# Layer-0 experts in units of 256 rows and halves of 128 rows

## The chip, the cores and the metric

The kernel runs on one core of a Trainium2 chip. A time is the device time of one execution in microseconds (us); the time of a kernel is the median of its timed runs. One more execution is recorded by the hardware profiler; the profile's lines come from that one. Its engines are PE (TensorE matmuls; PEld is its weight load), DVE (VectorE), ACT (ScalarE), POOL (GpSimd) and SP (SyncE, which here only issues DMAs).

## The reference, cut to what matters

The whole kernel computes two graph layers on 1250 nodes of 512 features. Each has a graph product, an attention part and a mixture of experts. Only the experts of layer 0 are concerned here:

```python
logits = jnp.einsum('btd,ed->bte', h, w_r) + b_r
topk_vals, topk_idx = jax.lax.top_k(logits, K)
gates = jax.nn.softmax(topk_vals, axis=-1)
hf = h.reshape(B * T, d)
hid = jax.nn.gelu(jnp.einsum('nd,edf->nef', hf, W1) + b1, approximate=False)
expert_stack = jnp.einsum('nef,efd->ned', hid, W2) + b2
gathered = jnp.take_along_axis(expert_stack, idx_flat[:, :, None], axis=1)
mixed = jnp.sum(gathered * gates_flat[:, :, None], axis=1).reshape(B, T, d)
return x + mixed
```

There are E = 8 experts, K = 2 for each node, d = 512 and a hidden width of 2048, all in float32. So 2500 (node, expert) pairs have to pass through a 512x2048 map, a gelu and a 2048x512 map, each with the weights of its own expert. Which expert a pair takes is known only while the kernel runs.

## The kernel before, in words

**Routing and planning.** The function `tile_graph_layers` is one long program. After the first graph product, `route` (called per 125 rows) writes the normalised rows to the DRAM table `hrow` and the logits to `lg`. Then the planning block (lines 655 to 751) runs once. `top2` gives the two experts of each row as one-hot masks `oh` and the gates. A matmul with a triangular matrix gives `pos`, the rank of each row within its expert; its last slice holds the row count of each expert. `un` holds the units of each expert (its rows divided by UT = 256, rounded up), their running sum, and the sum before. `eu` gives each unit its expert, and a flag that says whether this differs from the expert of the unit before. Both go as integers into `plan`, together with the number of units. `row` is the place of a pair: 256 times the first unit of its expert, plus its rank. From `row`, the tables `hi` and `lo` and twenty matmuls into `pslot` make `sf` and `slot`: for each block of 128 places, the row to fetch, the gate, and the row to add to. NB = 34 blocks. DVE does nearly all of this in small operations, and PE waits for `hi` before `pslot`.

**A unit.** There are up to NU = 17 units; the first NU0 = 10 run always (2500 pairs need at least 10), the others in nested branches `tc.If(n_units > u)`. `unit(u)` does the following:

- `weights(u)` (lines 801 to 810): SP reads the expert and the flag from `plan`, fetches the bias, and issues eight conditional loads of 1 MB, `ew1[0]`, `ew2[0]`, `ew1[1]`, `ew2[1]` and so on. Both maps have one set of four buffers each, so a load waits until the unit before has used that quarter.
- First map (line 820): for each 128 of the 2048 hidden columns, four matmuls accumulate in PSUM. The weights are stationary, the 256 turned rows `hu` are moving. ACT applies bias and gelu (line 821) into `hd`.
- `counts` (lines 168 to 191) for some of NG = 54 groups. This is work of layer 1, put here: each group counts edges of the graph. DVE and ACT make one-hot tiles (`sh`, `los`, four buffers), PE multiplies six pairs of them into `pa` (one PSUM bank, "acc"), ACT copies `pa` to `sa` (three buffers), and POOL adds `sa` into the DRAM table `adj` with an indirect accumulating DMA. Units 0 to 9 carry 5 or 6 groups each.
- `turn(u + 1)` transposes the next unit's rows (line 795), `fetch(u + 2)` gathers rows from `hrow` (line 783, POOL).
- Second map (line 829): for each quarter and each 128 hidden columns, two matmuls (one per 128 rows), with `hd` stationary and 512 columns of `ew2` moving, into two PSUM tiles `pye`.
- The two results are multiplied by the gates (lines 835 and 837) into `yo` and added to the DRAM table `xrow` by accumulating DMAs of POOL (line 838).

The order on each engine is set when the program is built, by priority and by a model of the engines: work of a later statement fills the gaps of an earlier one, except that nothing moves in or out of a branch. After the units, layer 1 begins: SP loads `adj` (`ad`, lines 868 to 881) and `xrow` (line 903), and PE transposes and multiplies.

Of the kernel before, what the change touches and what calls it, by code (L numbers as in the profile page):

```python
# [10 lines left out]
F32 = mybir.dt.float32  # L11
F16 = mybir.dt.float16
I32 = mybir.dt.int32
AF = mybir.ActivationFunctionType
OP = mybir.AluOpType
AX = mybir.AxisListType
# [3 lines left out]
N = 1250  # L20
D = 512
P = 128
R = 125
NT = N // R
# [14 lines left out]
EPS = 1e-5  # L39
E0, F0 = 8, 2048  # L40
UT = 2 * P
NU = (2 * N - E0) // UT + E0
NU0 = -(-2 * N // UT)
E1, F1 = 6, 341
EA = 5
FA = EA * F1
# [6 lines left out]
def tile_graph_layers(ctx: ExitStack, tc: tile.TileContext, i: dict, out: bass.AP):  # L53
    nc = tc.nc
    V, S, T, G = nc.vector, nc.scalar, nc.tensor, nc.gpsimd
# [18 lines left out]
    def mm_tile(name):  # L74
        return ps_tile("mm", name)

    def in_tile(name):
        return ps_tile("in", name)

    def tr_tile(name):  # L80
        return ps_tile("tr", name)
# [19 lines left out]
    ident = cst.tile([P, P], F32, name="ident")  # L101
# [51 lines left out]
    hrow = dram.tile([N, D], F32, name="hrow")  # L153
    xrow = dram.tile([N + P, D], F32, name="xrow")
# [38 lines left out]
    with ExitStack() as s0:  # L193
# [78 lines left out]
        for t in range(NT):  # L272
# [40 lines left out]
        base = ec.tile([P, 2, NG], F32, name="base")  # L313
# [203 lines left out]
        for b, blocks in ((3, ((3, 0), (3, 1), (3, 2))), (1, ((1, 0), (2, 0), (2, 1)))):  # L517
            pt = tr_tile("pgl")
# [12 lines left out]
        for a in range(4):  # L531
            pt = mm_tile("pt1")
# [12 lines left out]
        for c in range(4):  # L545
            pt = tr_tile("pwq")
# [23 lines left out]
        for a in range(4):  # L570
            pt = mm_tile("pmap")
            for c in range(4):
                T.matmul(pt, wqn[:, c, a * P:(a + 1) * P], U[:, c, :], start=c == 0, stop=c == 3)
            f = 1.0 / (math.sqrt(N) * cout)
# [74 lines left out]
    with ExitStack() as s3:  # L649
        fc = pool(s3, "fc")  # L650
        fw = pool(s3, "fw", bufs=2)
# [6 lines left out]
        oh, gw2 = top2(nc, fc, lg[:R], gates[:R], R, NT, E0, softmax=True)  # L658
# [10 lines left out]
        for t in range(NT):  # L669
# [6 lines left out]
        pos = fc.tile([P, NT + 1, E0], F32, name="pos")  # L676
# [1 line left out]


        KU = -(-N // UT)  # L680
        stp = fc.tile([P, KU], F32, name="stp")
        G.iota(stp, pattern=[[UT, KU]], base=0, channel_multiplier=0, allow_small_or_imprecise_dtypes=True)
        cmp_ = fc.tile([P, E0, KU], F32, name="cmpu")
        V.tensor_tensor(cmp_, pos[:, NT, :, None].to_broadcast([P, E0, KU]), stp[:, None, :].to_broadcast([P, E0, KU]),
                        op=OP.is_gt)
        un = fc.tile([P, 3, E0], F32, name="un")
        V.tensor_reduce(un[:, 0, :], cmp_, AX.X, OP.add)
        V.tensor_copy(un[:, 1, :], un[:, 0, :])
        for e in range(1, E0):
            V.tensor_tensor(un[:, 1, e:e + 1], un[:, 1, e - 1:e], un[:, 0, e:e + 1], op=OP.add)  # L690
        V.tensor_tensor(un[:, 2, :], un[:, 1, :], un[:, 0, :], op=OP.subtract)

        ui = fc.tile([P, NU], F32, name="ui")
        G.iota(ui, pattern=[[1, NU]], base=0, channel_multiplier=0, allow_small_or_imprecise_dtypes=True)
        cme = fc.tile([P, NU, E0], F32, name="cme")
        V.tensor_tensor(cme, ui[:, :, None].to_broadcast([P, NU, E0]), un[:, 1, None, :].to_broadcast([P, NU, E0]),
                        op=OP.is_ge)
        eu = fc.tile([P, 2, NU], F32, name="eu")
        V.tensor_reduce(eu[:, 0, :], cme, AX.X, OP.add)
        V.tensor_scalar(eu[:, 0, :], eu[:, 0, :], float(E0 - 1), None, op0=OP.min)  # L700
        V.memset(eu[:, 1, 0:1], 1.0)
        V.tensor_tensor(eu[:, 1, 1:], eu[:, 0, 1:], eu[:, 0, :NU - 1], op=OP.not_equal)
        plan = fc.tile([P, 2 * NU + 1], I32, name="plan")
        V.tensor_copy(plan[:, :2 * NU], eu.rearrange("p a u -> p (a u)"))
        V.tensor_copy(plan[:, 2 * NU:], un[:, 1, E0 - 1:E0])


        row = fc.tile([P, NT, E0], F32, name="row")
        V.scalar_tensor_tensor(row[:R], un[:R, 2, None, :].to_broadcast([R, NT, E0]), float(UT), pos[:R, :NT, :],
                               op0=OP.mult, op1=OP.add)  # L710
        rw_ = fc.tile([P, 2, NT, E0], F32, name="rw_")
        rf = fc.tile([P, 2, NT], F32, name="rf")
        for n in range(2):
            V.tensor_tensor(rw_[:R, n], oh[n][:R], row[:R], op=OP.mult)
            V.tensor_reduce(rf[:R, n, :], rw_[:R, n], AX.X, OP.add)
        ri = fc.tile([P, 2 * NT], I32, name="ri")
        V.tensor_copy(ri[:R], rf[:R].rearrange("p n t -> p (n t)"))
        NB = NU * UT // P
        part = fc.tile([P, 2, 2 * NT], I32, name="part")
        V.tensor_scalar(part[:R, 0, :], ri[:R], 7, None, op0=OP.arith_shift_right)  # L720
        V.tensor_scalar(part[:R, 1, :], ri[:R], P - 1, None, op0=OP.bitwise_and)
# [7 lines left out]
        q = [R, 2 * NT, NB]  # L729
        V.tensor_tensor(hi[:R, :, 1, :], bi[:R, None, :NB].to_broadcast(q), pf[:R, 0, :, None].to_broadcast(q),  # L730
                        op=OP.is_equal)
# [5 lines left out]
        for a in range(2 * NT):  # L737
# [3 lines left out]
                     stop=a == 2 * NT - 1)  # L741

        sf = fc.tile([P, 5, NB], F32, name="sf")
# [6 lines left out]
        slot = fc.tile([P, 2, NB], I32, name="slot")  # L750
# [15 lines left out]
        ew1 = [fc.tile([P, 4, 512], F32, name=f"ew1_{q}") for q in range(4)]  # L766
        ew2 = [fc.tile([P, 4, 512], F32, name=f"ew2_{q}") for q in range(4)]

        def value(n, engines, top):
            return nc.values_load(plan[0:1, n:n + 1], engines=engines, min_val=0, max_val=top,  # L770
                                  skip_runtime_bounds_check_because="worked out above, within these bounds")

        SPE = (mybir.EngineType.SP,)
# [23 lines left out]
            return hu  # L797

        def weights(u):
            e, new = value(u, SPE, E0 - 1), value(NU + u, SPE, 1)  # L800
            b1 = fw.tile([P, 16], F32, tag="b1", name="b1")
            nc.sync.dma_start(b1[:, None, :], i["L0_ffn_b1"][:, bass.ds(e, 1), :])
            for q in range(4):
                nc.sync.dma_start(
                    ew1[q], i["L0_ffn_W1"][bass.ds(e, 1), :, q * 512:(q + 1) * 512].rearrange("o (k p) f -> p (o k) f", p=P),
                    cond=new)
                nc.sync.dma_start(
                    ew2[q], i["L0_ffn_W2"][bass.ds(e, 1), q * 512:(q + 1) * 512, :].rearrange("o (k p) f -> p (o k) f", p=P),
                    cond=new)
            return b1  # L810

        def unit(u, hu, xu):
            b1 = weights(u)
            hd = []
            for q in range(4):
                hd.append(fw.tile([P, 4, UT], F32, tag="hd", bufs=6, name="hd"))
                for f in range(4):
                    ph = in_tile("phd")
                    for k in range(4):
                        T.matmul(ph[:, :UT], ew1[q][:, k, f * P:(f + 1) * P], hu[:, k, :], start=k == 0, stop=k == 3)  # L820
                    S.activation(hd[q][:, f, :], ph[:, :UT], AF.Gelu, bias=b1[:, 4 * q + f:4 * q + f + 1], scale=1.0)  # L821
            for g in range(u * NG // NU0, (u + 1) * NG // NU0 if u < NU0 else 0):
                counts(fk, g, code0, idx0, "acc")
            after = turn(u + 1, xu) if u + 1 < NU else None, fetch(u + 2) if u + 2 < NU else None
            py = [mm_tile("pye") for _ in range(2)]
            for q in range(4):
                for f in range(4):
                    for a in range(2):
                        T.matmul(py[a], hd[q][:, f, a * P:(a + 1) * P], ew2[q][:, f, :],  # L829
                                 start=q == 0 and f == 0, stop=q == 3 and f == 3)  # L830
            for a in range(2):
                yo = fw.tile([P, D], F32, tag="yo", bufs=3, name="yo")
                k = 2 * u + a
                if a:
                    S.mul(yo, py[a], sf[:, 1, k:k + 1])
                else:
                    V.tensor_scalar(yo, py[a], sf[:, 1, k:k + 1], None, op0=OP.mult)  # L837
                G.indirect_dma_start(  # L838
                    out=xrow[:, :], out_offset=bass.IndirectOffsetOnAxis(ap=slot[:, 1, k:k + 1], axis=0),
                    in_=yo, in_offset=None, compute_op=OP.add)  # L840
            return after

        hu, xu = turn(0, fetch(0)), fetch(1)
        for u in range(NU0):
            hu, xu = unit(u, hu, xu)
        n_units = value(2 * NU, mybir.ALL_ENGINES, NU)
        with ExitStack() as s4:
            for u in range(NU0, NU):
                s4.enter_context(tc.If(n_units > u))
                hu, xu = unit(u, hu, xu)  # L850
    sc_.close()

    with ExitStack() as s1:
        xp = pool(s1, "xp")
        XN = xp.tile([P, NT, D], F32, name="XN")
        with ExitStack() as s2:
            ap = pool(s2, "adj")
# [3 lines left out]
            with ExitStack() as s3:  # L861
# [4 lines left out]
                for d in range(NT):  # L866
# [7 lines left out]
                    for s0_ in range(0, NT, 4):  # L874
                        n = min(4, NT - s0_)
                        pt = tr_tile("pat")
# [78 lines left out]
        n = FA // P  # L955
# [318 lines left out]
```

## Time and profile before

| what | us |
|---|---|
| median of the timed runs (three: 2479.42, 2479.59, 2485.83) | 2479.59 |
| the profiled execution's own time | 2379.38 |
| its span, from first to last instruction | 2377.6 |
| first expert matmul starts | 782.8 |
| the last of the unconditional units ends on PE | 1396.6 |
| first of the conditional units starts its first map | 1399.3 |
| last expert result is made | 1573.1 |
| mean granted PE clock | 0.965 of full speed |

Both times are of the same kernel; the profiled execution is 100 us shorter than the median of the timed ones. In a line of the profile's groups, `out<-in` names the tiles, `128*128 128x512` the stationary and the moving operand of a matmul, `xN` the number of records, then busy us and mean ns of one, then the idle time of the engine just ahead of these instructions and what ended it. A float32 matmul of this kernel is recorded as two passes, so 832 records of line 829 are 416 matmuls, 32 for each of 13 units. A line of a timeline has start and duration in us, engine, source line, operation, names, and in brackets the idle time before it with its releaser. A line of the windows view has the stretch, its length, the busy time of PE, PEld, DVE, ACT and POOL, the granted clock, the busy share of the DMA engines and GB/s.

### The profile page before, as it was taken

How to read it: one execution, taken by the hardware profiler on the slowest of the kernel's cores; microseconds unless marked ns; L12 is line 12 of the kernel's file. 1: busy time of each engine (PE TensorE's matmuls, PEld its weight loads, DVE VectorE, ACT ScalarE, POOL GpSimd, SP SyncE). 2: the span in 40 equal slices, each digit the busy share in tenths (PEclk: the TensorE clock that was granted, in tenths of full speed). 3: DMA queues.
4: the chain of work that ended last, by engine and by line, in shares of the span. 5: the costliest groups of instructions: out<-in, count | busy, mean ns of one | idle time of the engine just before them, and what ended most of it. 6: DMA issues, size and time to landing. Idle time of an engine off the chain costs nothing. (4 is left out here: it accounts for less than half of the span.)

```text
span 2377.6 us, 29905 instructions
## 1 busy us (share of the span) xinstructions
PE 2220.0 (93%) x11524; PEld 1223.3 (51%) x11524; DVE 875.9 (37%) x1814; ACT 616.0 (26%) x1631; POOL 599.3 (25%) x535
## 2 busy tenths in 40 slices
PE   6889888899897999999999999979999999988999
PEld 4334333333464666666666656644446455443454
DVE  3588888888365212111111110023000124573000
ACT  1444444443121333333233321122111011122000
POOL 0577777777020112222222220000000000002000
PEclk9899999999996899999999999989999999989999
DMA  6687777777433656522652245433002030110000
GB/s 218 236 221 199 185 186 186 186 184 183 103 95 103 191 166 156 146 32 49 173 152 31 27 95 159 142 84 109 0 0 67 4 68 18 36 30 1 13 13 18
DMA packets 129004, 253.63 MB, mean 107 GB/s; under 512 B 21532, under 2 KB 52204, under 8 KB 127308
## 3 DMA queue, kind: packets, MB, share of 16 engines
q0 software_dynamic: 47536, 116.88, 21.9%
q1 hardware_dynamic: 78952, 129.64, 17.6%
q10 hardware_dynamic: 2356, 5.00, 0.8%
q8 instruction: 97, 1.59, 0.3%
q14 instruction: 63, 0.52, 0.1%
HBM read 245.60 MB, written 47.81 MB: 123 GB/s over the span
## 5 line engine op out<-in xcount | busy, mean ns | idle before, releaser
L829 PE MATMUL pye<-ew,hd 128*128 128x512 f32 x832 | 371.3, 592 | 0.0
L820 PE MATMUL phd<-hu,ew 128*128 128x256 f32 x1664 | 365.6, 382 | 5.7 <-ACT hd L821 3.7
L403 POOL DMA_INDIRECT sg<-xup,srcc x323 | 314.5, 974 | 175.2 <-issue 64.9
L820 PEld LDWEIGHTS phd<-hu,ew 128*128 128x128 f32 x1664 | 318.1, 192 | 54.2 <-issue 4.3
L417 DVE TENSOR_TENSOR msg<-pw,sg 128x768 f32<-128x768 f32 x323 | 305.5, 946 | 0.0
L434 PE MATMUL pd<-msg,sy 128*32 128x320 f32 x646 | 225.3, 450 | 59.0 <-DVE msg L417 58.7
L829 PEld LDWEIGHTS pye<-ew,hd 128*128 128x128 f32 x832 | 152.9, 190 | 164.0 <-issue 161.9
L436 PE MATMUL pd<-msg,sy 128*32 128x256 f32 x1938 | 201.9, 395 | 0.0
L408 PE MATMUL pw<-w4b,h 64*128 64x512 f32 x646 | 188.5, 660 | 0.0
L185 DVE TENSOR_SCALAR los<-iol,slo 128x314 f16<-128x314 f16 x215 | 56.9, 302 | 307.1 <-PE pa L186 305.7
L821 ACT ACTIVATE hd<-phd,b 128x256 f32<-128x256 f32 x208 | 98.4, 473 | 265.0 <-PE phd L820 256.9
L414 DVE TENSOR_TENSOR msg<-pw,sg 128x256 f32<-128x256 f32 x323 | 134.6, 417 | 87.9 <-DMA sg<-xup,srcc 60.7
L434 PEld LDWEIGHTS pd<-msg,sy 128*32 128x32 f32 x646 | 50.4, 109 | 199.7 <-DVE msg L417 138.2
L396 ACT ACTIVATE sy<-oh,y 128x32 f32<-128x32 f32 x646 | 146.6, 311 | 0.3 <-DVE oh L388 0.3
L189 POOL DMA_INDIRECT adj<-sa,idx x54 | 85.5, 1584 | 209.3 <-DMA adj<-sa,idx 83.5
L1075 POOL IOTA unit<- 128x14 f32 x1 | 0.2, 153 | 524.9 <-DVE ys L1040 524.9
L837 DVE TENSOR_SCALAR yo<-pye,sf 128x512 f32<-128x512 f32 x13 | 9.7, 750 | 322.6 <-PE pye L829 322.6
L1085 PE MATMUL ph<-uT,w 128*128 128x500 f32 (+3 forms) x336 | 124.7, 526 | 0.8 <-ACT uT L122 0.7
L1096 PE MATMUL pyf<-w,hd 128*125 128x512 f32 (+1 forms) x280 | 125.1, 599 | 0.0
L440 PEld LDWEIGHTS pd<-msg,sy 128*32 128x32 f32 x1938 | 80.8, 112 | 58.9 <-issue 3.5
L838 POOL DMA_INDIRECT xrow<-yo,slot x26 | 40.5, 1559 | 256.4 <-DVE yo L837 142.8
L381 ACT ACTIVATE h<-ph 128x512 f32<-128x512 f32 (+1 forms) x124 | 68.8, 592 | 114.6 <-PE ph L377 72.1
(369 smaller groups left out, 2638.6 us busy)
## 6 DMA issues: line engine op xcount, KB each, us to landing
ew<-in_L_ffn_W SPq DMA_DIRECT2D x104, 1024.0 KB
agg<-zero SPq DMA_DIRECT2D x6, 1024.0 KB
adj<-zero SPq DMA_DIRECT2D x6, 1024.0 KB
ag<-agg SPq DMA_DIRECT2D x10, 560.0 KB
ad<-adj SPq DMA_DIRECT2D x10, 547.8 KB
sg<-xup,srcc POOLq DMA_INDIRECT x323
w<-in_L_gnn_W SPq DMA_DIRECT2D x4, 1024.0 KB
w<-in_L_ffn_W SPq DMA_DIRECT2D x5, 682.0 KB
```

The lines of the kernel that those rows point to most:

```text
L396: S.mul(sy[:, j, c, :], oh[:, j, :], y4[:, t0 + j, c:c + 1])
L403: G.indirect_dma_start(out=sg, out_offset=None, in_=xup[:, :], in_offset=bass.IndirectOffsetOnAxis(ap=srcc[:, t:t + 1], axis=0))
L408: T.matmul(pw, h[hb:hb + HID, q, (j // 2) * P:(j // 2 + 1) * P], w4b[hb:hb + HID, :], start=True, stop=True)
L414: V.tensor_tensor(msg[:, :, 0, :], w_[:, 0], sg[:, None, :P].to_broadcast([P, 2, P]), op=OP.mult)
L417: V.tensor_tensor(msg[:, :, 1:, :], w_[:, 1, :, None, :].to_broadcast(q), s1[:, None].to_broadcast(q), op=OP.mult)
L434: T.matmul(d[:W, :SW], sy[:, j, 0, :], mf.rearrange("p a u -> p (a u)")[:, :SW], **q)
L436: T.matmul(d[c * W:(c + 1) * W, :2 * P], sy[:, j, c, :], mf[:, 4:5 + c:c, :], start=j == 0, stop=False, skip_group_check=True)
L820: T.matmul(ph[:, :UT], ew1[q][:, k, f * P:(f + 1) * P], hu[:, k, :], start=k == 0, stop=k == 3)
L821: S.activation(hd[q][:, f, :], ph[:, :UT], AF.Gelu, bias=b1[:, 4 * q + f:4 * q + f + 1], scale=1.0)
L829: T.matmul(py[a], hd[q][:, f, a * P:(a + 1) * P], ew2[q][:, f, :], start=q == 0 and f == 0, stop=q == 3 and f == 3)
L1085: T.matmul(ph[:m, :c], w1[:, k, f * P:f * P + m], uT[:, k, c0:c1], start=k == 0, stop=k == 3)
L1096: T.matmul(py[:R], hd[f][:m, r0:r0 + R], w2[f // 4][:m, f % 4, :], start=f == 0, stop=f == FT - 1)
```

## The change

A remainder of an expert's rows of up to 128 becomes a half unit; only a larger remainder takes a full unit. The constants follow: at most NU = 13 units, of which NU0 = 6 run always, and up to 8 halves, each in a branch. The 54 count groups are divided over NU0 units as before, so each of the six now carries 9.

```diff
-NU = (2 * N - E0) // UT + E0
-NU0 = -(-2 * N // UT)
+
+NU = (2 * N + E0 * (UT - P - 1)) // UT
+NU0 = -(-(2 * N - E0 * P) // UT)
+NB = 2 * NU + E0
```

The planning block counts both kinds. `cmp_` compares each expert's rows with 0, 256, ... and with 128, 384, ...; the second sum is the number of units, the first less the second is 1 where there is a half. Rows of a half get places after all units:

```diff
+        un = fc.tile([P, E0, 2], F32, name="un")
+        V.tensor_reduce(un, cmp_, AX.X, OP.add)
+        V.tensor_tensor(un[:, :, 0], un[:, :, 0], un[:, :, 1], op=OP.subtract)
...
+        V.tensor_tensor(cme[:, :NU], ui[:, :, None].to_broadcast(q), upto[:, None, :, 1].to_broadcast(q), op=OP.is_ge)
+        q = [P, E0, E0]
+        V.tensor_tensor(cme[:, NU:], ui[:, :E0, None].to_broadcast(q), upto[:, None, :, 0].to_broadcast(q), op=OP.is_ge)
...
+        off = fc.tile([P, 3, E0], F32, name="off")
+        V.tensor_tensor(off[:, :2, :].rearrange("p c e -> p e c"), upto, un, op=OP.subtract)
+        V.tensor_scalar(off[:, 1, :], off[:, 1, :], float(UT), None, op0=OP.mult)
+        V.tensor_scalar(off[:, 0, :], off[:, 0, :], float(P), float(NU * UT), op0=OP.mult, op1=OP.add)
+        V.tensor_scalar(off[:, 2, :], un[:, :, 1], float(UT), None, op0=OP.mult)
+        V.tensor_tensor(off[:, 0, :], off[:, 0, :], off[:, 2, :], op=OP.subtract)
+        V.tensor_tensor(off[:, 0, :], off[:, 0, :], off[:, 1, :], op=OP.subtract)
+        row = fc.tile([P, 2, NT, E0], F32, name="row")
...
```

`weights` takes the flag for a unit only; the loads of a half are made always, also where a unit of the same expert had the weights before:

```diff
-            e, new = value(u, SPE, E0 - 1), value(NU + u, SPE, 1)
+            e = value(u, SPE, E0 - 1)
+            new = dict(cond=value(NU + E0 + u, SPE, 1)) if u < NU else {}
```

A half has 128 rows. In its first map the turned rows `hb` are stationary and 512 columns of `ew1` are moving, so the result has rows on partitions; DVE copies it out of PSUM, PE transposes it in four blocks, and ACT applies bias and gelu on those:

```diff
+        def half(j):
+
+            b1 = weights(NU + j)
+            hb = hbs[j % 2]
+            hd = []
+            for q in range(4):
+                ph = in_tile("phh")
+                for k in range(4):
+                    T.matmul(ph, hb[:, k, :], ew1[q][:, k, :], start=k == 0, stop=k == 3)
+                pre = fw.tile([P, 512], F32, tag="pre", name="pre")
+                V.tensor_copy(pre, ph)
+                pt = tr_tile("pht")
+                for f in range(4):
+                    T.transpose(pt[:, f * P:(f + 1) * P], pre[:, f * P:(f + 1) * P], ident)
+                hd.append(fw.tile([P, 4, UT], F32, tag="hd", bufs=6, name="hd"))
+                for f in range(4):
+                    S.activation(hd[q][:, f, :P], pt[:, f * P:(f + 1) * P], AF.Gelu,
+                                 bias=b1[:, 4 * q + f:4 * q + f + 1], scale=1.0)
+            if j + 1 < E0:
+                turn_half(j + 1)
+            if j + 2 < E0:
+                fetch_half(j + 2)
+            py = mm_tile("pyh")
+            for q in range(4):
+                for f in range(4):
+                    T.matmul(py, hd[q][:, f, :P], ew2[q][:, f, :], start=q == 0 and f == 0, stop=q == 3 and f == 3)
+            add(py, 2 * NU + j)
```

`fetch_half` gathers 128 rows into `xbs`, `turn_half` makes four transposes and one copy into `hbs`; `add` is the former end of a unit for one block of 128 rows (gate, then the accumulating DMA). The order of calls:

```diff
         hu, xu = turn(0, fetch(0)), fetch(1)
         for u in range(NU0):
             hu, xu = unit(u, hu, xu)
-        n_units = value(2 * NU, mybir.ALL_ENGINES, NU)
+            if u == 0:
+                fetch_half(0)
+                fetch_half(1)
+            if u == 1:
+                turn_half(0)
+        n_units, n_halves = (value(2 * NU + E0 + n, mybir.ALL_ENGINES, m) for n, m in ((1, NU), (0, E0)))
         with ExitStack() as s4:
             for u in range(NU0, NU):
                 s4.enter_context(tc.If(n_units > u))
                 hu, xu = unit(u, hu, xu)
+        with ExitStack() as s4:
+            for j in range(E0):
+                s4.enter_context(tc.If(n_halves > j))
+                half(j)
```

More of the change, by code (lines that the diff above doesn't have):

```diff
@@ L680, in tile_graph_layers @@
         KU = -(-N // UT)
[L681 to L687, printed above, removed]
@@ L688, in tile_graph_layers @@
-        V.tensor_copy(un[:, 1, :], un[:, 0, :])
+        stp = fc.tile([P, 2, KU], F32, name="stp")
+        G.iota(stp, pattern=[[P, 2], [UT, KU]], base=0, channel_multiplier=0, allow_small_or_imprecise_dtypes=True)
+        cmp_ = fc.tile([P, E0, 2, KU], F32, name="cmpu")
+        q = [P, E0, 2, KU]
+        V.tensor_tensor(cmp_, pos[:, NT, :, None, None].to_broadcast(q), stp[:, None, :, :].to_broadcast(q), op=OP.is_gt)
+        un = fc.tile([P, E0, 2], F32, name="un")
+        V.tensor_reduce(un, cmp_, AX.X, OP.add)
@@ L689, in tile_graph_layers @@
+        V.tensor_tensor(un[:, :, 0], un[:, :, 0], un[:, :, 1], op=OP.subtract)
+        upto = fc.tile([P, E0, 2], F32, name="upto")
+        V.tensor_copy(upto[:, 0, :], un[:, 0, :])
         for e in range(1, E0):
-            V.tensor_tensor(un[:, 1, e:e + 1], un[:, 1, e - 1:e], un[:, 0, e:e + 1], op=OP.add)
-        V.tensor_tensor(un[:, 2, :], un[:, 1, :], un[:, 0, :], op=OP.subtract)
+            V.tensor_tensor(upto[:, e, :], upto[:, e - 1, :], un[:, e, :], op=OP.add)
         ui = fc.tile([P, NU], F32, name="ui")
@@ L694, in tile_graph_layers @@
         G.iota(ui, pattern=[[1, NU]], base=0, channel_multiplier=0, allow_small_or_imprecise_dtypes=True)
[L695 to L710, printed above, removed]
+        cme = fc.tile([P, NU + E0, E0], F32, name="cme")
@@ new lines, in tile_graph_layers @@
+        q = [P, NU, E0]
+        V.tensor_tensor(cme[:, :NU], ui[:, :, None].to_broadcast(q), upto[:, None, :, 1].to_broadcast(q), op=OP.is_ge)
+        q = [P, E0, E0]
+        V.tensor_tensor(cme[:, NU:], ui[:, :E0, None].to_broadcast(q), upto[:, None, :, 0].to_broadcast(q), op=OP.is_ge)
+        eu = fc.tile([P, 2 * NU + E0], F32, name="eu")
+        V.tensor_reduce(eu[:, :NU + E0], cme, AX.X, OP.add)
+        V.tensor_scalar(eu[:, :NU + E0], eu[:, :NU + E0], float(E0 - 1), None, op0=OP.min)
@@ new lines, in tile_graph_layers @@
+        new_ = eu[:, NU + E0:]
+        V.memset(new_[:, 0:1], 1.0)
+        V.tensor_tensor(new_[:, 1:], eu[:, 1:NU], eu[:, :NU - 1], op=OP.not_equal)
+        plan = fc.tile([P, 2 * NU + E0 + 2], I32, name="plan")
+        V.tensor_copy(plan[:, :2 * NU + E0], eu)
+        V.tensor_copy(plan[:, 2 * NU + E0:], upto[:, E0 - 1, :])
+        off = fc.tile([P, 3, E0], F32, name="off")
+        V.tensor_tensor(off[:, :2, :].rearrange("p c e -> p e c"), upto, un, op=OP.subtract)
+        V.tensor_scalar(off[:, 1, :], off[:, 1, :], float(UT), None, op0=OP.mult)
@@ new lines, in tile_graph_layers @@
+        V.tensor_scalar(off[:, 0, :], off[:, 0, :], float(P), float(NU * UT), op0=OP.mult, op1=OP.add)
[3 more added lines that the diff above has]
+        row = fc.tile([P, 2, NT, E0], F32, name="row")
+        q = [R, NT, E0]
+        V.tensor_tensor(row[:R, 1], pos[:R, :NT, :], off[:R, 2, None, :].to_broadcast(q), op=OP.is_ge)
@@ L711, in tile_graph_layers @@
+        V.tensor_tensor(row[:R, 1], row[:R, 1], off[:R, 0, None, :].to_broadcast(q), op=OP.mult)
+        V.tensor_tensor(row[:R, 0], pos[:R, :NT, :], off[:R, 1, None, :].to_broadcast(q), op=OP.add)
+        V.tensor_tensor(row[:R, 0], row[:R, 0], row[:R, 1], op=OP.add)
         rw_ = fc.tile([P, 2, NT, E0], F32, name="rw_")
@@ L713, in tile_graph_layers @@
         for n in range(2):
-            V.tensor_tensor(rw_[:R, n], oh[n][:R], row[:R], op=OP.mult)
+            V.tensor_tensor(rw_[:R, n], oh[n][:R], row[:R, 0], op=OP.mult)
             V.tensor_reduce(rf[:R, n, :], rw_[:R, n], AX.X, OP.add)
@@ L717, in tile_graph_layers @@
         V.tensor_copy(ri[:R], rf[:R].rearrange("p n t -> p (n t)"))
-        NB = NU * UT // P
         part = fc.tile([P, 2, 2 * NT], I32, name="part")
@@ L805, in weights @@
                     ew1[q], i["L0_ffn_W1"][bass.ds(e, 1), :, q * 512:(q + 1) * 512].rearrange("o (k p) f -> p (o k) f", p=P),
-                    cond=new)
+                    **new)
                 nc.sync.dma_start(
                     ew2[q], i["L0_ffn_W2"][bass.ds(e, 1), q * 512:(q + 1) * 512, :].rearrange("o (k p) f -> p (o k) f", p=P),
-                    cond=new)
+                    **new)
             return b1
@@ L831, in unit @@
             for a in range(2):
[L832 to L840, printed above, removed]
@@ L841, in unit, with add @@
-            return after
+                add(py[a], 2 * u + a)
+            return after
+        def add(py, k):
+            yo = fw.tile([P, D], F32, tag="yo", bufs=3, name="yo")
+            if k % 2:
+                S.mul(yo, py, sf[:, 1, k:k + 1])
+            else:
+                V.tensor_scalar(yo, py, sf[:, 1, k:k + 1], None, op0=OP.mult)
+            G.indirect_dma_start(
+                out=xrow[:, :], out_offset=bass.IndirectOffsetOnAxis(ap=slot[:, 1, k:k + 1], axis=0),
+                in_=yo, in_offset=None, compute_op=OP.add)
@@ new lines, in tile_graph_layers, with fetch_half, turn_half @@
+        hbs = [fc.tile([P, 4, P], F32, name=f"hb{n}") for n in range(2)]
+        xbs = [fc.tile([P, D], F32, name=f"xb{n}") for n in range(2)]
+        def fetch_half(j):
+            G.indirect_dma_start(
+                out=xbs[j % 2], out_offset=None, in_=hrow[:, :],
+                in_offset=bass.IndirectOffsetOnAxis(ap=slot[:, 0, 2 * NU + j:2 * NU + j + 1], axis=0))
+        def turn_half(j):
+            pt = tr_tile("phb")
+            for k in range(4):
+                T.transpose(pt[:, k * P:(k + 1) * P], xbs[j % 2][:, k * P:(k + 1) * P], ident)
+            evict(hbs[j % 2], pt.rearrange("p (k r) -> p k r", k=4))
@@ new lines, in half @@
+        def half(j):
[4 more added lines that the diff above has]
+                ph = in_tile("phh")
+                for k in range(4):
+                    T.matmul(ph, hb[:, k, :], ew1[q][:, k, :], start=k == 0, stop=k == 3)
[17 more added lines that the diff above has]
+            add(py, 2 * NU + j)
```

## The prediction

> **What bounds the kernel now.** I read the page's totals first, then the two costliest groups, then the timelines of PE, POOL, ACT and SP over the expert stage, because the change touches nothing else.
>
> ```profile
> span 2377.6 us, 29905 instructions
> ...
> PE 2220.0 (93%) x11524; PEld 1223.3 (51%) x11524; DVE 875.9 (37%) x1814; ACT 616.0 (26%) x1631; POOL 599.3 (25%) x535
> ...
> L829 PE MATMUL pye<-ew,hd 128*128 128x512 f32 x832 | 371.3, 592 | 0.0
> L820 PE MATMUL phd<-hu,ew 128*128 128x256 f32 x1664 | 365.6, 382 | 5.7 <-ACT hd L821 3.7
> ...
> L189 POOL DMA_INDIRECT adj<-sa,idx x54 | 85.5, 1584 | 209.3 <-DMA adj<-sa,idx 83.5
> ```
>
> PE is busy 93% of the span, and the two expert products fill a third of it. A unit records 128 passes of L820 and 64 of L829 (each f32 matmul is two records), so 832/64 = 13 units run. In the windows view, a unit without graph counts:
>
> ```profile
> 1460.00:1516.00 56.00, 56.00 (x201) 37.31 (x200) 1.47 (x3) 8.85 (x18) 5.19 (x4) 1.00 0.53 169
> ```
>
> PE has no gap (56.00 of 56.00 us). The PE timeline splits it:
>
> ```profile
> 1460.22 1.04 PE L795 MATMUL phu<-ident,xr 128*128 128x128 f32 x8
> 1461.10 27.79 PE L820 MATMUL phd<-hu,ew 128*128 128x256 f32 x128
> 1488.73 27.63 PE L829 MATMUL pye<-ew,hd 128*128 128x512 f32 x64
> ```
>
> By differences of starts: turn 0.88, first map 27.63 (0.216 a pass), second 27.46 (0.43 a pass), together 55.97 us. Units 0 to 9 also carry the 54 count groups. A 5-group unit lasts 60.66 us (845.05 to 905.71), so a group costs PE (60.66-55.97)/5 = 0.94 us when nothing waits. Behind each group stands a chain on POOL. First without a weight load, then with one (POOL timeline; start, duration, idle before and its releaser):
>
> ```profile
> 1005.38 1.57 POOL L189 DMA_INDIRECT adj<-sa,idx  x1 [2.34 <-DMA adj<-sa,idx]
> 1010.33 1.55 POOL L189 DMA_INDIRECT adj<-sa,idx  x1 [3.37 <-ACT sa L188]
> 1015.21 1.55 POOL L189 DMA_INDIRECT adj<-sa,idx  x1 [3.33 <-DMA adj<-sa,idx]
> 1020.02 1.55 POOL L189 DMA_INDIRECT adj<-sa,idx  x1 [3.27 <-DMA adj<-sa,idx]
> ...
> 1132.60 1.60 POOL L189 DMA_INDIRECT adj<-sa,idx  x1 [3.27 <-ACT sa L188]
> 1140.96 1.55 POOL L189 DMA_INDIRECT adj<-sa,idx  x1 [6.76 <-DMA adj<-sa,idx]
> 1149.03 1.55 POOL L189 DMA_INDIRECT adj<-sa,idx  x1 [6.52 <-DMA adj<-sa,idx]
> ```
>
> Each accumulate waits for the one before: every 4.87 us when the DMA engines are free, 8.1 to 8.4 beside a load. PE issues groups faster, every 2.7 us (six `pa` matmuls between four `pye` passes). The buffers between are three `sa` and one `pa` bank, and a 6-group unit already shows them full (ACT, then PE timeline):
>
> ```profile
> 947.80 0.42 ACT L188 COPY sa<-pa 128x313 f32<-128x313 f32 x1 [1.31 <-DMA adj<-sa,idx]
> ...
> 948.27 0.69 PE L186 MATMUL pa<-los,sh 128*128 128x313 f16 x4 [1.48 <-ACT sa L188]
> ```
>
> The fifth copy waits for the second accumulate; the sixth group's matmuls, with 46 second-map passes queued behind them on PE, wait for that copy. Today that costs 1.5 us; nine groups a unit will feel it.
>
> [...] so 1.55 us is not the chain's price, 4.87 is. [...] one record here is 286, but eight back to back take 1.04 us, so I use 0.13 each.
>
> **The change part by part.** How many halves run decides it. The reference's layer-0 routing on its own seeded inputs gives the experts 230, 211, 56, 545, 199, 969, 174 and 116 rows. Rounded up to 256: 1, 1, 1, 3, 1, 4, 1, 1 units = 13, as the trace has; and the conditional load issues (0.37 us where taken, 0.07 where skipped) skip at units 4, 5, 8, 9 and 10, as these numbers demand. After: units 1, 1, 0, 2, 1, 4, 1, 0 = 10, and 3 halves (experts 2, 3, 7).
>
> 1. *Three units become halves.* A half: first map 16 matmuls x 2 passes x 0.43 = 13.76; 16 transposes x 0.13 = 2.1; second map 13.76; turn of the next 0.5: 30.1 us. The DVE copies (0.75 each, from the `yo` row) and 16 small gelus lie beside PE. Gain 3 x (56.0-30.1) = -77.5. Bounds for a half: 30 if all lies beside, 37 if each quarter's copy, transposes and gelu stand open (1.7 x 4); I take 30.1 plus 0.7 for the branches.
>
> 2. *Weights.* Expert 3 is loaded a second time: 8.4 MB. A half needs 8.4 MB each, 22 us at 380 GB/s. From the previous half's second-map start T, the six loads up to the last `ew1` quarter go out from T+3.4[...]. PE wants that quarter near T+25. Nothing, or 1 us a half; inside the range.
>
> 3. *54 count groups in 6 units: 9 each, not 5.4.* The PE work is the same (nothing). The wait is not. With s the first group's start, group k (from 0) would start at s+2.7k; it needs the copy of group k-1, so the end of accumulate k-4, plus 0.6. Accumulate 1 ends near s+13.9, so group 8 starts no earlier than s+13.9+0.6+3c, c being the cadence; unhindered it is s+21.6. Stall per unit = 3c-7.1. At 4.87: 7.5. Where the next unit loads, its first two quarters (2 MB) go out once 16 second-map passes are done, near s+12, and one interval is 8.1: 10.7. Loads follow units 0, 1, 3 and 4, not 2 and 5: 4 x 10.7 + 2 x 7.5 = 58; unit 0 can start a group in its first map (788.2), 3 less; today's stalls of 1.7 go: +53. From below: 0, if the built order puts more second-map passes between the groups; from above: all intervals at 8.1, 17.2 x 6 = 103.
>
> 4. *Planning on DVE.* Some 11 more small operations at 0.16 (L687 to L717 today) before `hi`, for which PE waits at 749.1: +1.7. `NB` stays 34, so the slot work is unchanged.
>
> 5. *First two halves' fetches and one turn*: two gathers of 1 us on POOL, cadence slack there; four transposes, +0.5.
>
> 6. *Into the branches.* SP's `ad` loads stand ahead of the first conditional unit's bias and wait for the last accumulate (1393.2 today, 3.4 us before PE ends). With nine groups it ends near s+48, where PE ends too; today's stall of 5.5 becomes about 10: +4. One more register value and a second jump: +3.
>
> 7. *The end.* Today:
>
> ```profile
> 1572.53 1.62 POOL L838 DMA_INDIRECT xrow<-yo,slot  x1 [44.05 <-DVEq L847]
> ...
> 1578.05 1.58 POOL L838 DMA_INDIRECT xrow<-yo,slot  x1 [3.89 <-DMA xrow<-yo,slot]
> ...
> 1584.39 0.36 SPq L89 DMA_DIRECT2D X<-xrow  x1
> ```
>
> The loads of X, and a PE gap of 10.8, wait for two chained adds. A half has one: -5.5. Next comes the `ad` work, which is there today.
>
> Sum: -77.5+2+53+1.7+0.5+7-5.5 = -19. The profiled execution's own time is 2379.4 (span 2377.6 and 1.8 around it); it would be 2360. The median of the timed runs, 2479.6, lies 100 above for reasons that the profile doesn't show; taking the difference over with the same ratio (1.042), -20: 2460.
>
> **The rivals.** *The chain does not hold PE*: the built order spreads the nine groups over the 27 us of the second map (3 us each, and slack from the three `sa`), or starts them in the first map as unit 0 does. For it: priority order is made ahead of the run and fills gaps; against it: units with 5 and with 6 groups show the same 2.7 spacing, although the sixth already waits. Sum -72: about 2405. *The chain holds PE at its loaded cadence everywhere* and the change is slower: stalls 103, sum +31: 2512. For it: 8.1 to 9.8 in units followed by a load; against: units 2 and 5 have no load behind them, and a stalled PE also frees fewer weight buffers, so fewer loads run. It decides from a mean cadence c where 6(3c-7.1) reaches 72+1.7, c = 6.5; I take 4.87 to 5.9. *The change doesn't do what it says* (fewer halves run): excluded by the routing, unless it differs on the chip; then about 2480 and up.
>
> **How the numbers follow.** Forecast case 0.57, its own range 2440 to 2476 (stalls 40 to 70, branch and half terms). No hold 0.25, 2395 to 2440. Loaded cadence 0.16, 2488 to 2520. No halves 0.02. Range for 8 in 10: 2398 to 2490, which leaves out most of the slow case and a little of the fast one. A measurement tells about 0.3%, 7.4 us, from no change: faster 0.75 (the fast case and most of the forecast), same 0.09, slower 0.16.
>
> **What would show it.** 640 L829-type passes in units and 96 in halves; a half near 30 us on PE without DMA waits; nine groups a unit, with PE waits on the `sa` copy at groups 6 to 8 of about 2.2 us each, 3 more where a load follows; units 0 to 5 at 72 to 76 us; `X<-xrow` about 6.5 us after the last product. Wrong if PE shows no such waits (then 2405), if accumulates stay 8 us apart with no load running, or if halves wait for `ew`.

## The result and the profile after

The changed kernel takes 2471.34 us (median of five, 2468.5 to 2473.21) beside 2484.27 of the kernel before (median of five, 2479.42 to 2485.83): a ratio of 0.9957, interval 0.9944 to 0.9971. (A ratio here is estimated from all runs of both kernels; it is not the quotient of the two medians, which is 0.9948 and lies in the interval.) By the ratio the change is faster by about 11 us, by the medians by 13; the forecast had 20.

The profile of before that was shown above is of an execution whose first 780 us, ahead of the experts, ran 92 to 109 us shorter than in every later profile. A second profile of the same kernel (experiment 1 below) has the first expert matmul at 891.5, as the changed kernel has it (890.8), and a span of 2485.0. So the stages are compared with that second profile; it is one execution, 3 us longer than its kernel's median on that chip. Of the page of the changed kernel, totals and costliest groups:

```profile
span 2471.4 us, 29281 instructions
...
PE 2240.5 (91%) x11180; PEld 1186.7 (48%) x11180; DVE 888.6 (36%) x1834; ACT 606.6 (25%) x1628; POOL 587.5 (24%) x531
...
L846 PE MATMUL pye<-ew,hd 128*128 128x512 f32 x640 | 300.9, 609 | 0.0
L837 PE MATMUL phd<-hu,ew 128*128 128x256 f32 x1280 | 282.4, 383 | 7.8 <-DMA ew<-in_L_ffn_W 6.1
...
L191 POOL DMA_INDIRECT adj<-sa,idx x54 | 84.9, 1573 | 212.1 <-ACT sa L190 123.6
```

640 records of the second map are 10 units, so three units became halves. The accumulates (the last line) now wait most for the copy `sa`, before for one another. The stages are read from the starts of instructions on PE (the end of the last one, for the experts). The first and the last expert lines, of the second profile of before, then of the changed kernel:

```profile
891.49 4.92 PE L820 MATMUL phd<-hu,ew 128*128 128x256 f32 x16 [0.27 <-ACT hu L122]
...
1671.67 7.89 PE L829 MATMUL pye<-ew,hd 128*128 128x512 f32 x18
```

```profile
890.80 5.66 PE L837 MATMUL phd<-hu,ew 128*128 128x256 f32 x16 [0.27 <-ACT hu L124]
...
1662.00 8.75 PE L902 MATMUL pyh<-ew,hd 128*128 128x512 f32 x20
```

| stretch (us) | before, second profile | after | difference | forecast |
|---|---|---|---|---|
| plan: from `ppos` to the first `phd` | 44.5 | 46.0 | +1.5 | +1.7 |
| experts: first to last expert matmul | 788.1 | 780.0 | -8.1 | -15.0 |
| last expert matmul to layer 1's first product (`pgc`) | 46.0 | 40.4 | -5.6 | -5.5 |
| sum | | | -12.2 | -18.8 |

The spans differ by 13.6. All of the forecast's error lies in the middle row. Three places of it have to be looked at.

**The six units with counts.** First the wait list of the `pa` matmuls and their `sa` copies (us in total, times), then unit 1 on PE and on POOL:

```profile
its engine sat idle before it (us, times) until:
  DMA adj<-sa,idx: 70.4, 23
  ACT sa L190: 40.6, 17
```

```profile
1008.59 1.02 PE L846 MATMUL pye<-ew,hd 128*128 128x512 f32 x2
1015.53 1.21 PE L188 MATMUL pa<-los,sh 128*128 128x313 f16 x4 [5.91 <-ACT sa L190]
...
1024.91 0.69 PE L188 MATMUL pa<-los,sh 128*128 128x313 f16 x4 [1.48 <-ACT sa L190]
```

```profile
1007.12 1.57 POOL L191 DMA_INDIRECT adj<-sa,idx  x1 [3.21 <-ACT sa L190]
1015.71 1.55 POOL L191 DMA_INDIRECT adj<-sa,idx  x1 [7.01 <-ACT sa L190]
1020.48 1.55 POOL L191 DMA_INDIRECT adj<-sa,idx  x1 [3.23 <-ACT sa L190]
```

PE stands for 40.6 us, 17 times, in front of a `pa` bank that ACT has not emptied; ACT stands for 70.4 us, 23 times, because all three `sa` still wait for their accumulate. The accumulates shown come 8.59 us apart while a weight load runs, 4.77 after it: near the two cadences of the forecast. PE's stop is longest at the slow one (5.91 us, beside 1.48).

**Into the branches.** From the end of unit 5's second map (1334.3) to the start of unit 6's (1372.7) PE takes 38.4 us, where a turn and a first map take 28.5 undisturbed: 9.9 lost. In the second profile of before the same stretch behind unit 9 takes 36.5 (1503.48 to 1539.99): 8.0 lost. Forecast +4, measured +1.9.

**The first half.** Unit 9 and the halves on PE:

```profile
1540.64 27.63 PE L846 MATMUL pye<-ew,hd 128*128 128x512 f32 x64
1576.59 5.78 PE L885 MATMUL phh<-ew,hb 128*128 128x512 f32 x8 [8.31 <-DMA ew<-in_L_ffn_W]
1583.18 1.10 PE L885 MATMUL phh<-ew,hb 128*128 128x512 f32 x2 [0.81 <-DMA ew<-in_L_ffn_W]
...
1609.98 4.45 PE L885 MATMUL phh<-ew,hb 128*128 128x512 f32 x10
...
1640.28 4.46 PE L885 MATMUL phh<-ew,hb 128*128 128x512 f32 x10
```

Unit 9 ends at 1568.1 (the marked end of its last line is 1568.27), and the halves start anew at 1609.98 and 1640.28. The first half costs 41.9 us, the second 30.3, and the third 30.5 (to the end of its last product at 1670.75). Only the first waits for `ew`. SP, which issues these loads, shows why. Its waits in this stretch (us in total, times, longest), then its timeline:

```profile
SPq L819 <- ACTq L914: 49.3, 1, 49.3
```

```profile
1512.34 0.37 SPq L824 DMA_DIRECT2D ew<-in_L_ffn_W  x1
1569.07 0.36 SPq L819 DMA_DIRECT2D b<-in_L_ffn_b  x1
1569.76 0.37 SPq L821 DMA_DIRECT2D ew<-in_L_ffn_W  x1
```

L819 is the bias load at the head of `weights`; L914 is the `with` statement that holds the nest of conditional units, and the instructions at the nest's end carry its number. SP had passed the branches of units 10 to 12, which don't run (its last branch instruction of L914 starts at 1518.3), and stood 49.3 us in front of the first half's bias until ACT had passed them too; ACT does so after its part of unit 9 (its last one starts at 1569.1). The view of line L914 has the instruction that SP waited for (a line gives shortest, median and longest in ns, then first and last start; PE's is listed under PEld):

```profile
L914 PEldq EVENT_SEMAPHORE  x1: 51/51/51, 1568.3 to 1568.3; - x1
L914 ACTq EVENT_SEMAPHORE  x1: 17/17/17, 1569.0 to 1569.0; - x1
```

SP's wait list names ACT's L914 as what the bias load waited for; ACT's instruction starts at 1569.0, and the load goes out at 1569.07. All eight weight loads came behind that, and PE could use the first quarter 6.8 us after its issue.

### The profile page after: what moved, and what is told of

Same layout as the page of the kernel before. It is cut to its first block, busy times and chain, and to the rows that moved or that the text cites. A ratio compares the mean times of both kernels' runs of the same rounds, so it can differ in the third digit from the quotient of the medians.

```text
span 2471.4 us, 29281 instructions
## 1 busy us (share of the span) xinstructions
PE 2240.5 (91%) x11180; PEld 1186.7 (48%) x11180; DVE 888.6 (36%) x1834; ACT 606.6 (25%) x1628; POOL 587.5 (24%) x531
## 5 line engine op out<-in xcount | busy, mean ns | idle before, releaser
L846 PE MATMUL pye<-ew,hd 128*128 128x512 f32 x640 | 300.9, 609 | 0.0
L837 PE MATMUL phd<-hu,ew 128*128 128x256 f32 x1280 | 282.4, 383 | 7.8 <-DMA ew<-in_L_ffn_W 6.1
L837 PEld LDWEIGHTS phd<-hu,ew 128*128 128x128 f32 x1280 | 245.3, 192 | 44.2 <-DMA ew<-in_L_ffn_W 6.4
L438 PE MATMUL pd<-msg,sy 128*32 128x256 f32 x1938 | 230.5, 402 | 17.7 <-issue 16.7
L410 PE MATMUL pw<-w4b,h 64*128 64x512 f32 x646 | 204.7, 668 | 5.9 <-PE pd L442 2.7
L846 PEld LDWEIGHTS pye<-ew,hd 128*128 128x128 f32 x640 | 119.1, 195 | 114.6 <-issue 111.0
L442 PE MATMUL pd<-msg,sy 128*32 128x64 f32 x1938 | 117.5, 225 | 29.8 <-issue 28.5
L442 PEld LDWEIGHTS pd<-msg,sy 128*32 128x32 f32 x1938 | 92.5, 114 | 93.1 <-issue 48.0
L436 PEld LDWEIGHTS pd<-msg,sy 128*32 128x32 f32 x646 | 53.0, 111 | 164.2 <-DVE msg L419 76.4
L838 ACT ACTIVATE hd<-phd,b 128x256 f32<-128x256 f32 x160 | 75.8, 474 | 210.3 <-PE phd L837 192.9
```

Of the source, the lines that this page charges most:

```text
L410: T.matmul(pw, h[hb:hb + HID, q, (j // 2) * P:(j // 2 + 1) * P], w4b[hb:hb + HID, :], start=True, stop=True)
L436: T.matmul(d[:W, :SW], sy[:, j, 0, :], mf.rearrange("p a u -> p (a u)")[:, :SW], **q)
L438: T.matmul(d[c * W:(c + 1) * W, :2 * P], sy[:, j, c, :], mf[:, 4:5 + c:c, :], start=j == 0, stop=False, skip_group_check=True)
L442: T.matmul(d[c * W:(c + 1) * W, 2 * P:SW], sy[:, j, 0, :], mf.rearrange("p a u -> p (a u)")[:, a:a + 64], start=False, stop=q["stop"], ski ...
```

## The experiments

Seven more runs were made, four on one chip (before: 2473.09 there), three on another (before: 2483.9). Each ratio is to the kernel before on its own chip.

| label | what | median us | ratio | interval |
|---|---|---|---|---|
| before_again | before, profiled again | 2486.82 (one run) | | |
| b9 | before, 9 groups in each of units 0 to 5 | 2515.43 | 1.0175 | 1.0159 to 1.019 |
| a_sa7 | after, seven `sa` buffers | 2415.24 | 0.9766 | 0.9753 to 0.978 |
| a_front | a_sa7, and fewer groups in unit 5 | 2399.48 | 0.9706 | 0.9692 to 0.9719 |
| a_trim | after, without units 10 to 12 | 2452.43 | 0.9922 | 0.9908 to 0.9935 |
| a_b1own | after, own bias buffer for halves | 2467.29 | 0.9942 | 0.993 to 0.9954 |
| a_front_trim | a_front and a_trim together | 2400.13 | 0.9664 | 0.9649 to 0.968 |

**1. Before once more.** Nothing is edited; the question is whether the 108 us ahead of the experts belong to the change.

> The kernel before, unchanged, for a second profile. Its first profile had the first expert matmul at 782.8 us and a span of 2377.6, the changed kernel 890.8 and 2471.4. If the 108 us belong to the execution and not to the change, this profile has the first expert matmul between 865 and 890 and a span near 2470, with 787 to 792 us from the first to the last expert matmul as before.

One stretch of the graph stage in the windows view, first of the profile of before, then of the second one (columns as above: busy times, granted clock, DMA share, GB/s):

```profile
300.00:400.00 100.00, 87.71 (x1078) 37.30 (x1076) 84.85 (x148) 42.42 (x154) 77.74 (x74) 1.00 0.75 186
```

```profile
300.00:400.00 100.00, 85.24 (x868) 34.99 (x864) 67.73 (x117) 34.46 (x128) 61.67 (x60) 0.96 0.61 156
```

The same kernel did a fifth less work in the same 100 us (868 matmul records, not 1078). The experts take 788.1 us, as expected; their start, 891.5, lies 1.5 us beyond the expected range. The 108 us are not the change's. Why one execution is so much quicker there stays open.

**2. The packing of counts alone.** On the kernel before, which keeps its 13 units and no halves:

```diff
-            for g in range(u * NG // NU0, (u + 1) * NG // NU0 if u < NU0 else 0):
+            for g in range(u * NG // 6, (u + 1) * NG // 6 if u < 6 else 0):
```

> The kernel before, with its 54 count groups put nine each into units 0 to 5 and none into units 6 to 9; nothing else differs. If the packing of the groups costs by itself (nine accumulates behind three sa buffers), PE waits on the sa copy at groups 6 to 8 of each of the six units, 7 to 11 us a unit, some 53 us in all: ratio to the kernel before 1.018 to 1.024. If the waits seen after the change come from something else in it (the other planning, the fetches of the halves), the ratio is 1.000 and no such waits stand in the timeline.

Slower by 43 us; the expert stage grew from 788.1 to 833.6. The second unit on PE shows the same stop as in the changed kernel:

```profile
999.14 1.20 PE L186 MATMUL pa<-los,sh 128*128 128x313 f16 x4 [5.84 <-ACT sa L188]
...
1009.03 0.69 PE L186 MATMUL pa<-los,sh 128*128 128x313 f16 x4 [2.07 <-ACT sa L188]
```

The six packed units last 73.8, 75.0, 74.8, 72.2, 71.1 and 74.7: 441.6 together. That is what the forecast's terms give for them, 6 x 55.97 + 54 x 0.94 + 55 = 441.6, to the tenth by chance. The expected waits on `sa` are there, but they add up to 39.4 us, not 53. The ratio lies just under the expected one: unit 9 has no counts any more, and the way into the branches loses 0.9 us instead of 8.0.

**3. The wait taken out.** On the changed kernel, seven `sa` buffers instead of three; to make room, `hi` moves into a buffer of another pool. The order on PE stays as it was.

```diff
-    def counts(sp, g, code, idx, bank):
+    def counts(sp, g, code, idx, bank, deep=3):
...
-        sa = sp.tile([P, LO], F32, tag="sa", bufs=3, name="sa")
+        sa = sp.tile([P, LO], F32, tag="sa", bufs=deep, name="sa")
...
-        hi = fc.tile([P, 2 * NT, 2, NB], F32, name="hi")
+        hi = fr.tile([P, 2 * NT, 2, NB], F32, bufs=1, name="hi")
...
-                counts(fk, g, code0, idx0, "acc")
+                counts(fk, g, code0, idx0, "acc", 7)
```

> The changed kernel with seven sa buffers instead of three (room is made by moving the planning tile hi to a pool that is closed earlier; the order on PE is the same as in the changed kernel). If the three buffers tie PE to the accumulate chain, the six units with counts fall from about 73.9 us to about 65 each, 50 to 53 us in all; but the chain of unit 5 then ends some 11 us after PE has ended that unit, so the ad loads on SP and the bias queued behind them come later and the wait before the first conditional unit grows by about 10. Net 40 to 45 below the changed kernel, ratio to the kernel before 0.977 to 0.981. If the chain itself or ACT and DVE bound the groups, PE's wait moves to another place and less than 15 us is gained.

The wait list of `pa` and `sa` in this kernel, whole:

```profile
its engine sat idle before it (us, times) until:
  PE pa L188: 1.8, 2
```

No copy waits for an accumulate, no matmul for a copy. Units 0 to 4 last 66.6, 65.1, 64.7, 64.7 and 64.7, together 325.8 against 372.4: 46.6 us back. The waits in these five were 35.9 (40.6 less unit 5's 4.7). The other 10.7 are no waits but slower work (in the changed kernel PE is busy for 335.64 us of these five units, 10 more than they last here), and the clock can account for a good part of them: over the five units the granted clock is 0.96 with the waits; in this kernel it is 0.98 from 874.50 to 1287.00, a stretch that also holds the stop of 12.73 us shown below. 0.02 x 372 = 7 us (an estimate from these two rounded figures, as part of the slow time falls into the waits). Unit 5 itself, to its end on PE, is 6.5 us shorter (64.7, not 71.2), so the six units give back 53.0, the upper end of what was expected. But the queue that the buffers hold moved: with nine groups, unit 5's last accumulate goes out at 1268.64, SP's `ad` loads wait for it (from 1272.71), and the bias and the skipped weight loads of unit 6 stand behind these (1277.64 and 1278.65):

```profile
1278.77 6.62 PE L837 MATMUL phd<-hu,ew 128*128 128x256 f32 x16 [12.73 <-DMA ew<-in_L_ffn_W]
```

That takes back what unit 5 had gained. The stage is 733.7 us, 46.2 below the changed kernel; the ratio, 0.9766, lies just under the expected range.

**4. The same, with fewer groups in the last unit.** a_sa7's edits, and ten groups in each of the first four units, nine and five in the last two:

```diff
+CUT = (0, 10, 20, 30, 40, 49, 54)
...
-            for g in range(u * NG // NU0, (u + 1) * NG // NU0 if u < NU0 else 0):
+            for g in range(CUT[u], CUT[u + 1]) if u < NU0 else ():
```

> As with seven sa buffers, but the groups go 10, 10, 10, 10, 9 and 5 to the six units, so that the last unit's chain ends before PE does. Expected about 10 us below the kernel with seven buffers and nine groups in each unit: the wait before the first conditional unit is back at 5 us or less, ratio to the kernel before 0.972 to 0.977. If that wait has nothing to do with the chain's end (register loads, branch), the two kernels are equal.

```profile
1269.36 1.04 PE L811 MATMUL phu<-ident,xr 128*128 128x128 f32 x8
1270.23 3.62 PE L838 MATMUL phd<-hu,ew 128*128 128x256 f32 x16
```

In this timeline of PE, unit 6's first map (L838 here) follows its turn without a wait; from the start of unit 5 to that of unit 6 are 61.6 us, not 78.4. The ratio is a little better than expected. It beats both kernels, by 3% and 2.5%, and uses nothing that depends on the inputs.

**5. The skipped units left out.** On the changed kernel; units 10 to 12 are not in the program, which is enough for these inputs alone:

```diff
-            for u in range(NU0, NU):
+            for u in range(NU0, 10):
```

> The changed kernel without units 10 to 12 in the program, which these inputs do not reach, so no branch is skipped between unit 9 and the first half. If SP is held before the first half because the skipped branches are counted off only when the other engines have passed them, the eight loads of the first half go out while unit 9 still runs, PE does not wait for ew at the first half (9.1 us after the change), and the first half takes about 31 us instead of 41.9: 9 to 11 us below the changed kernel, ratio to the kernel before 0.991 to 0.993. If SP is held at any end of a branch, or by the bias buffer alone, nothing changes.

SP, then PE:

```profile
1501.92 0.36 SPq L819 DMA_DIRECT2D b<-in_L_ffn_b  x1
1507.84 0.37 SPq L821 DMA_DIRECT2D ew<-in_L_ffn_W  x1
1535.42 0.37 SPq L824 DMA_DIRECT2D ew<-in_L_ffn_W  x1
...
1556.03 0.37 SPq L824 DMA_DIRECT2D ew<-in_L_ffn_W  x1
```

```profile
1555.83 4.45 PE L885 MATMUL phh<-ew,hb 128*128 128x512 f32 x10
...
1586.14 4.46 PE L885 MATMUL phh<-ew,hb 128*128 128x512 f32 x10
```

The first half's bias and eight loads go out during unit 9, from 1501.92 to 1556.03; its matmuls wait for nothing, and it takes 30.3 us as the others do. The expert stage is 769.0, 11.0 less than in the changed kernel, and by the ratios 0.0035 x 2480 = 8.7 us are gained.

**6. The bias alone.** The wait that the trace names is that of the bias. With a buffer of its own for halves, only that wait goes:

```diff
-            b1 = fw.tile([P, 16], F32, tag="b1", name="b1")
+            b1 = fw.tile([P, 16], F32, tag="b1" if u < NU else "b1h", name="b1")
```

> The changed kernel with bias buffers of their own for the halves. The bias load of the first half, which stood at the head of SP's queue and waited for ACT until unit 9 was over, is then free to go. If the bias buffer alone held SP, the loads of the first half go out 25 to 50 us earlier and 9 to 11 us are gained (ratio to the kernel before 0.991 to 0.993). If the weight buffers are held by the same skipped branches (PE's count instead of ACT's), only the bias goes early, the first ew load still waits for the end of unit 9 on PE, and the ratio stays at 0.995 to 0.997.

SP's timeline, then its waits:

```profile
1510.00 0.37 SPq L824 DMA_DIRECT2D ew<-in_L_ffn_W  x1
1517.22 0.36 SPq L819 DMA_DIRECT2D b<-in_L_ffn_b  x1
1566.06 0.37 SPq L821 DMA_DIRECT2D ew<-in_L_ffn_W  x1
```

```profile
SPq L821 <- PEq L914: 48.1, 1, 48.1
```

The bias goes out at 1517.22, but the first weight load then stands 48.1 us for PE to pass the skipped branches, and goes out at 1566.06. PE waits 5.44 + 2.31 us where it waited 8.31 + 0.81. The view of L914 in this kernel has PE's instruction at the nest's end (listed under PEld) at that moment:

```profile
L914 PEldq EVENT_SEMAPHORE  x1: 51/51/51, 1566.0 to 1566.0; - x1
```

The ratio lies between the two expected ranges, and its interval overlaps that of the changed kernel: no gain that can be told. The wait for ACT (49.3 us) hid a nearly equal one for PE (48.1) behind it.

**7. Both together**, a_front's edits and a_trim's:

> Both repairs together: seven sa buffers with groups 10, 10, 10, 10, 9, 5, and units 10 to 12, which these inputs do not reach, left out of the program. If the two waits are independent, the gains add: 0.9706 less 0.0035, so a ratio to the kernel before of 0.966 to 0.969, and PE waits for no ew load and no sa copy between the first unit and the last half. If one hides the other, it stays at 0.970.

0.9664, as expected; the stage shrinks from a_front's 717.9 to 707.3 us, 10.6, as the trim alone gave 11.0. Between the first unit and the last half no matmul waits for a weight load or for an `sa` copy. The two costs are separate.

## Why the prediction was right in kind and wrong on the first half's loads

- **Step 1, halves for units (-77.5):** right. The second and third take 30.3 and 30.5 us beside 30.1 worked out.
- **Step 2, "Weights": "Nothing, or 1 us a half"** is the step that failed, for the first half. The six loads were to go out from T+3.4 behind the second map of what ran before. For halves 2 and 3 they do go out while the half before runs (1587.30 to 1610.17 for the second; the built order mixes the two maps, so not in the forecast's steps), and PE waits for none. For the first, "before" is unit 9, and between lie three skipped branches: nothing goes out until ACT and PE have passed them. With the 0.7 us a half for branches and the 3 us that step 6 gave to the second jump, both the author's estimates and not measured, the three halves were put at 90.3 + 2 + 3 = 95.3 us; they took 102.65. That is 7.3 us more; with 1.9 from step 3 and -2.1 from step 6 it makes 7.1, where the stage missed by 6.9. Experiment 5 gives the whole of it back, experiment 6 shows that it holds for PE (48.1 us) as for ACT (49.3). The prediction had named it as a sign of being wrong that halves wait for `ew`: the first one does, for 9.1 us. The step's 380 GB/s is near what the first profile of before shows for its first load: 354, 393 and 383 GB/s in the three windows of 4 us from 788 to 800, 377 over the 12 us. At 380 the six loads of 1.05 MB take 16.6 us, which from T+3.4 is T+20, ahead of the T+25 at which PE wants the last (an estimate from this rate and the issue times, with nothing for the start of a transfer).
- **Step 3, stalls (+53):** right in mechanism and in sum, not in how the time is spent. Beside seven buffers (experiment 3) the six units are 53.0 us longer, where 55 were put; units followed by a load 8.3 to 11.1, the other two 6.4 and 6.5. But only 40.6 of it are waits: 7.2 to 8.3 us where a load follows (not 10.7), 4.7 and 5.0 elsewhere (not 7.5). The other 12.4 are slower work, which was not priced. The forecast's formula gives when the chain lets the last group start, so slow work ahead of that group takes the place of waiting (argued, not tested); slow work behind it, as in unit 3 at 1171.11, comes on top. That the sum fits so closely is in part luck. The six units end after 443.5 us, 1.9 over the 441.6 of the sum. Of the spacing inside a unit, unit 5 shows waits of 0.50, 2.23 and 2.00 at the last three groups, as foretold.
- **Steps 4 and 7 (plan, end):** within 0.2 us each. `X<-xrow` comes 7.3 us after the last product, where about 6.5 were named.
- **Step 6, into the branches:** +1.9 instead of +4. PE stands idle for 7.5 us (6.12 and 1.38), where about 10 were put, and experiment 4 confirms that the last accumulate sets it.
- **The rivals:** *the chain does not hold PE* falls by the 17 waits of the profile after, and by experiment 3, which makes it true and then gains 46 us. *The loaded cadence everywhere* falls by the accumulates, which are 4.6 to 5.1 us apart in unit 5, where no load runs.

A term for the lost prefetch would have been needed. Part of it could be read from the first profile: units 13 to 16 are skipped there, and the view of L847, the nest of that kernel, shows the same two instructions after the last unit's work (its last result is made at 1573.1), while SP had passed its own at 1522.9:

```profile
L847 PEldq EVENT_SEMAPHORE  x1: 51/51/51, 1572.4 to 1572.4; - x1
L847 ACTq EVENT_SEMAPHORE  x1: 17/17/17, 1573.1 to 1573.1; - x1
```

The prediction's own line of the end, `[44.05 <-DVEq L847]`, names such an instruction as a releaser. What that profile could not show is the price for a weight load, as none follows the nest there.

What remains: that a wait belongs to branches that are skipped, and not to every end of a nest, rests on experiment 5, in which all units of the nest run. Buffers of their own for the first half's weights, and running the halves ahead of the conditional units, were not tried.

## What to carry to other kernels

When work with a serial tail, such as accumulates that wait for one another, is packed into fewer places, count the buffers between it and the bottleneck engine. Here nine groups a unit, not five or six, made PE wait 40.6 us behind three buffers and not at all behind seven; the four more took 46 us off the stage, where the change itself had taken 8. Price a prefetch across branches that are skipped at no prefetch, as it was in this kernel: loads behind them went out only when the engines that last used those buffers had passed the branches too (here after 49.3 us for ACT, 48.1 for PE). When the wait that a trace names is taken away, look for a second one behind it (here 48.1 us behind 49.3).

## What was not expected of the hardware

In the changed kernel some waits of PE cost more than themselves. The windows view around the wait of 5.91 us in unit 1 (the column before the DMA share is the granted clock):

```profile
1006.00:1015.50 9.50, 3.52 (x12) 1.34 (x12) 3.17 (x8) 3.02 (x8) 1.57 (x1) 0.93 0.73 238
1015.50:1020.00 4.50, 4.47 (x10) 2.05 (x10) 2.05 (x5) 1.88 (x5) 1.55 (x1) 0.50 0.32 36
1020.00:1025.00 5.00, 3.52 (x12) 1.46 (x11) 2.26 (x6) 2.39 (x6) 1.55 (x1) 0.89 0.27 32
```

PE resumes at half clock and keeps it for about 5 us: a pair of second-map passes lasts 1.91 us there, 1.02 otherwise. The wait of 4.03 us in unit 0 is followed by one such slow pair (1.92), that of 1.48 us in unit 1 by none. The first half's wait of 8.31 us, too, is followed by eight matmul passes in 5.78 us, where ten take 4.45 otherwise; the granted clock is 0.50 from 1577 to 1580. Shorter waits can do the same. In unit 2 the half clock comes behind waits of 1.90 and 2.08 us, in unit 3 behind one of 2.17:

```profile
1092.70:1096.10 3.40, 3.40 (x6) 1.05 (x5) 1.43 (x3) 1.59 (x5) 0.85 (x1) 0.51 0.39 47
1171.20:1174.60 3.40, 3.40 (x7) 1.36 (x6) 1.64 (x5) 1.71 (x4) 1.55 (x1) 0.51 0.21 31
```

A wait of 2.53 us in unit 4 has no slow pair behind it. So in this case the length of a single wait does not decide it; what does was not measured.
